# Two queues for the adjacency tiles of a graph network's first range, with the feature quarters behind them

## The chip, the cores and the metric

The kernel runs on one core of one Trainium2 chip. The metric is the time of one execution on the device in microseconds (us). It took 2988.14 us before the change (median of three runs, 2979.09 to 2988.84).

## The reference, cut to what matters

Four graph layers run over a dense 2708 x 2708 adjacency matrix (mostly zeros) and 2708 x 512 features, each with a residual and a layer norm. The change touches only how layer 0 starts:

```python
def _L0_gnn_ref(cur, incidence_m):
    mask = incidence_m > 0
    head = mask.astype(incidence_m.dtype)
    head = head / jnp.maximum(jnp.sqrt(jnp.sum(head * head, axis=-1, keepdims=True)), EPS)
    inc = incidence_m + head                      # needs the count of a whole row first
    edge_fea = inc @ cur
    edge_degree = jnp.sum(inc, axis=-1, keepdims=True)
    return edge_fea / edge_degree
...
x = _layernorm(x + _L0_gnn_ref(x, adj), axis=-1)  # layer 0; three more layers follow
```

What matters is the order of data. Before the first product of a row can be taken, the positive entries of that whole row have to be counted.

## The kernel before

The adjacency matrix is cut into four blocks "11", "12", "21", "22" of 1354 x 1354, and the features into four quarters B11, B12, B21, B22. Each block is worked on in ranges of up to 384 columns. The first range (256 columns) is `plain`, and for it a block has 11 tiles (ten of 128 rows and one of 74). Its loads, in the kernel before:

```python
def move(queue, dst, src):          # a tile's load; 74 rows go as 64 + 10, so 11 tiles are 12 issues
    ...
def load(ij, k, ...):
    ...
    move(nc.sync, t[:w, :n], adjT[j0 : j0 + w, hi * NH + R0 : hi * NH + R0 + n])
...
if plain:                           # (position in the list, length) of a block's 11 loads
    when = {"11": (-4.0, 0.2), "12": (-3.8, 0.2), "21": (-2.4, 0.4), "22": (-1.6, 0.4)}
    pw = {"11": (-0.9, 0.6), ...}   # the same for prep0 of each tile
```

The program is a list of events. `at(position, function)` enters one, the list is sorted by position, and each engine gets its instructions in the order that results. In the first part of the list this order is kept strictly; later events without the mark `True` may be taken earlier where nothing holds them.

The features of layer 0 and a bias vector of layer 1:

```python
def x0_load(k, s):
    if s == "B12":
        ...
        move(nc.sync, b12[k][: wt(k)], x_source(X0, k)[1])
    else:
        x_load(X0, k, s, nc.scalar if s == "B11" else nc.sync)
for k in range(KT):
    f = k / KT
    at(-5.0 + f, lambda k=k: x0_load(k, "B11"))
    at(-4.5 + 0.3 * f, lambda k=k: x0_load(k, "B21"))
    at(-4.0 + 0.3 * f, lambda k=k: x0_load(k, "B12"))
    ...
def start1():                       # layer 1; nothing holds it back, so the vector is loaded at the start
    W[1] = load_w(w_gcn)
    vec[1] = const.tile([P, D], F32, name="vec", tag="vec")
    nc.scalar.dma_start(out=vec[1], in_=bcast(b_gcn, D))
at(S[1] - 1.0, start1)
```

And the path from the tiles to the first product (h is the half of the rows, 0 first):

```python
for h, p, d in ((0, -3.7, 0.05), (1, 1.9, 0.055)):
    for i in range(NT):             # 22 tiles: 11 of block "h1", then 11 of "h2"
        at(..., lambda ...: count_mask(R0, n, h, i, a(), h == 0))   # h = 0 on VectorE, h = 1 on ScalarE
        at(..., lambda ...: count_tile(R0, n, h, i))                # TensorE: ones times mask
    at(..., lambda h=h: count_row(R0, n, h))                        # VectorE max, GpSimd power -1/2
    at(..., lambda h=h: spread_row(R0, n, h))

def spread_row(R0, n, h):
    ...                             # TensorE spreads 1/sqrt(count) over 128 partitions
    nc.scalar.copy(row[R0, h][:, :n], pr[:, :n])
def prep0(r, R0, n, h, hj, k, a):   # inc = adj + mask * row
    nc.vector.scalar_tensor_tensor(t[:w, :n], a[:w, :n], 0.0, row[R0, h][:w, :n], ALU.is_gt, ALU.mult)
    nc.vector.tensor_tensor(a[:w, :n], a[:w, :n], t[:w, :n], ALU.add)
```

GpSimd issues the count loads of the next range (`cl`, 192 KB each); it issues the first seven of them right after its part of `count_row`.

Of the kernel before, what the change touches and what calls it, by code (L numbers as in the profile page):

```python
# [27 lines left out]
NH = 1354  # L28
# [22 lines left out]
def wt(k):  # L51
    return min(P, NH - k * P) if k < KT else P
# [8 lines left out]
def gnn_kernel(ctx: ExitStack, tc: tile.TileContext, x, adjT, w_sa, a_sa, w_gcn, b_gcn, wab, bab, w_hop, w_out,  # L61
               b_out, out):
    nc = tc.nc
# [40 lines left out]
    X0 = [x[h * NH + k * P : h * NH + k * P + wt(k), :] for h in range(2) for k in range(KT)]  # L104
# [18 lines left out]
    def move(queue, dst, src):  # L123

        m = dst.shape[0]
        c = m - m % 16 if m > 16 else m
        queue.dma_start(out=dst[:c], in_=src[:c])  # L127
        if c < m:
            queue.dma_start(out=dst[c:m], in_=src[c:m])

    def ring_tile(nm):
        return pool.tile([P, 384], F32, name=nm, tag="ring", bufs=RING)
# [21 lines left out]
    def at(pos, fn, hold=False):  # L154

        def go():
            n = len(nc.cur_bb.bb.instructions)
            fn()
            held.update(range(n, len(nc.cur_bb.bb.instructions)))

        events.append((pos, len(events), go if hold else fn))
# [11 lines left out]
    def new_x(s, k):  # L173
        X[s, k] = place(s, *HOME[k])
        return X[s, k]
# [22 lines left out]
    def x_sums(k):  # L198
        w = wt(k)
        b = b12.pop(k)  # L200
        b11, b22 = X["B11", k], X["B22", k]
        nc.vector.tensor_tensor(new_x("T1", k)[:w], b[:w], b11[:w], ALU.subtract)
        nc.vector.tensor_tensor(new_x("T2", k)[:w], b22[:w], X["T1", k][:w], ALU.subtract)
        X["T3", k] = b
        nc.vector.tensor_tensor(b[:w], b22[:w], b[:w], ALU.subtract)
        X.pop(("B12", k), None)

    def x_last(k):
        w = wt(k)
        nc.vector.tensor_tensor(new_x("T4", k)[:w], X["B21", k][:w], X["T2", k][:w], ALU.subtract)  # L210

    def b12_tile(k):

        b12[k] = place("T3", *HOME[k])
        return b12[k]

    def x_source(src, k):

        lo, hi = src[k], src[KT + k]
        return lo[:, :HD], lo[:, HD:], hi[:, :HD], hi[:, HD:]  # L220

    def x_load(src, k, s, eng):
        w = wt(k)
        q = x_source(src, k)[("B11", "B12", "B21", "B22").index(s)]
        t = b12_tile(k) if s == "B12" else new_x(s, k)
        move(eng, t[:w], q)
# [74 lines left out]
    def sweep(base, nk, ranges, prep=None, extra=None, done=None, first=False, late=None, sums=False, save=False):  # L301
        A, spare = {}, {}
        for r, (R0, n) in enumerate(ranges):
            plain = first and r == 0
# [4 lines left out]
            def load(ij, k, R0=R0, n=n, r=r, plain=plain):  # L309
                hi, hj = int(ij[0]) - 1, int(ij[1]) - 1  # L310
                w = wt(k)
                if plain and ij == "22" and k >= KT - 8:

                    i = k - (KT - 8)
                    if i % 2 == 0:
                        spare[i // 2] = feat.tile([P, D], F32, name="aw", tag=f"w_{i // 2}")
                    t = spare[i // 2][:, i % 2 * HD : i % 2 * HD + n]
                else:
                    t = ring_tile("a" + ij)
                j0 = hj * NH + k * P  # L320
                move(nc.sync, t[:w, :n], adjT[j0 : j0 + w, hi * NH + R0 : hi * NH + R0 + n])
                A[r, ij, k] = t

            def prepare(ij, k, r=r, R0=R0, n=n):
# [13 lines left out]
            when = {"11": (-1.0, 1.0), "21": (-0.4, 1.0), "22": (0.75, 0.8), "12": (3.2, 1.0)}  # L338
            cw = {"s3": 0.3, "s1": 1.25, "s2": 2.1, "s4": 4.3}
            pw = {ij: (p + 0.3, f) for ij, (p, f) in when.items()}  # L340
            if plain:
                when = {"11": (-4.0, 0.2), "12": (-3.8, 0.2), "21": (-2.4, 0.4), "22": (-1.6, 0.4)}
                pw = {"11": (-0.9, 0.6), "12": (-0.3, 0.6), "21": (3.3, 0.9), "22": (4.1, 0.9)}
            for ij in ("11", "21", "22", "12"):
                for k in ks:
                    p, f = when[ij]
                    at(pb + p + f * k / nk, lambda ij=ij, k=k, load=load: load(ij, k))
                    if prep is not None:
                        p, f = pw[ij]
                        at(pb + p + f * k / nk, lambda ij=ij, k=k, prepare=prepare: prepare(ij, k))  # L350
            for k in ks if not plain else ():
                f = 0.75 * k / nk
# [305 lines left out]
    def x0_load(k, s):  # L658
        if s == "B12":
            X["B12", k] = b12_tile(k)  # L660
            move(nc.sync, b12[k][: wt(k)], x_source(X0, k)[1])
        else:
            x_load(X0, k, s, nc.scalar if s == "B11" else nc.sync)

    for k in range(KT):
        f = k / KT
        at(-5.0 + f, lambda k=k: x0_load(k, "B11"))
        at(-4.5 + 0.3 * f, lambda k=k: x0_load(k, "B21"))
        at(-4.0 + 0.3 * f, lambda k=k: x0_load(k, "B12"))
        at(-3.0 + 0.3 * f, lambda k=k: x0_load(k, "B22"))  # L670
        at(6.2 + 0.9 * f, lambda k=k: x_sums(k))
        at(7.5 + f, lambda k=k: x_last(k))
    at(9.3, start0)
    sweep(S[0], KT, RANGES0, prep=prep0, extra=extra0, done=done0, first=True, sums=True)


# [102 lines left out]
    def done1(p0, dp, last, R0, n, h, C, tiles):  # L779
        for i, (t, lo, w) in enumerate(tiles):  # L780
# [13 lines left out]
            at(p0 + 0.25 + dp * i, b)  # L794

    sweep(S[1], KT, RANGES, extra=extra1, done=done1, late=0.85, save=True)

    eps_col = const.tile([P, NT], F32, name="eps_col")
# [44 lines left out]
    def done2(p0, dp, last, R0, n, h, C, tiles):  # L843
        gots = []
        for i, (t, lo, w) in enumerate(tiles):
# [44 lines left out]
            at(q + 0.5 + 0.6 * dp * i, f)  # L890

    sweep(S[2], KT, RANGES, prep=prep2, extra=extra2, done=done2, sums=True)


# [332 lines left out]
```

## Time and profile before

| of the kernel before | value | where it is read |
|---|---|---|
| TensorE busy | 98% of 2983.9 us | busy times of the page |
| last mask of the first row ends | 19.50 us | timeline, the group at 18.94 |
| ScalarE's last load issue ends | 10.28 us | timeline |
| row copied on ScalarE | 21.61 us | timeline |
| first matmul of the layer | 22.95 us | timeline |
| second range starts | 120.50 us | timeline, the first matmul into `accu` |

TensorE is the bound for all but the start. The prediction below shows these lines; read them as one chain, in which each bracket names what the engine waited for. In them, `ACTq` is ScalarE's sequencer, which issues loads; `ACT` is its compute part. The two share one stream of instructions in order. `ACT_TABLE_LOAD`, called the table load here, stands once before ScalarE's first compute instruction and takes 1.28 us. PSUM is the memory in which TensorE's results lie.

### The profile page before, as it was taken

The page shows a single profiled execution, that of the slowest core. Times are in us where ns is not written, and L with a number is a line of the kernel's source. Part 1 is how long each engine was busy: PE and PEld are TensorE (multiplying, and loading weights), DVE is VectorE, ACT ScalarE, POOL GpSimd, SP SyncE. Part 2 cuts the span into 40 slices and gives each one's busy share as a digit, 9 for nine tenths or more (in the row PEclk, how much of TensorE's full clock was granted, in tenths as well). Part 3 has the DMA queues.
Part 4 walks back from the last instruction along what each step waited for, and adds up shares of the span by engine and source line. Part 5 has one row for each costly group of instructions (what it writes and reads, how often), then busy time and mean ns, then how long its engine had stood idle before and what let it go on. Part 6 is the DMA issues. An engine that isn't in the chain of part 4 may idle for free.

```text
span 2983.9 us, 37755 instructions
## 1 busy us (share of the span) xinstructions
PE 2930.5 (98%) x10982; PEld 1926.6 (65%) x10982; DVE 2191.4 (73%) x5376; ACT 596.3 (20%) x1145; POOL 692.6 (23%) x1240
## 2 busy tenths in 40 slices
PE   7999999999999999999999999999999999999998
PEld 6655666557665657766666666666666666665664
DVE  5889688556657675874686777867768877689786
ACT  4544200000144444551101000010000100100001
POOL 1423224233410101213112022020220322512112
PEclk9999999999999999999999999999999999999999
DMA  7665467586754333654676667565675666875562
GB/s 233 199 198 176 143 179 217 141 136 138 192 113 124 110 112 94 202 158 143 199 218 212 183 194 219 169 208 178 196 225 174 196 200 197 242 199 179 172 177 83
DMA packets 364119, 524.27 MB, mean 176 GB/s; under 512 B 57734, under 2 KB 312430, under 8 KB 363912
## 3 DMA queue, kind: packets, MB, share of 16 engines
q1 hardware_dynamic: 297556, 362.80, 43.4%
q0 software_dynamic: 57040, 148.22, 16.1%
q10 hardware_dynamic: 9316, 10.84, 1.2%
q8 instruction: 87, 1.43, 0.2%
q14 instruction: 120, 0.98, 0.1%
HBM read 431.26 MB, written 90.37 MB: 175 GB/s over the span
## 4 chain that ended last, share of the span: by engine, by line
PE 84%; issue 5%; DVE 4%; DMA 4%; ACT 1%; POOL 1%; SPq 1%; POOLq 0%; DVEq 0%; ACTq 0%
PE accc L1007 12%; PE accd L1007 12%; PE accu L1007 12%; PE ps_d L495 9%; PE accu L367 8%; PE accc L367 8%; PE accd L367 7%; PE acca L1007 6%; PE acca L367 4%; PE ps_n L1076 1%; PE accc L1012 1%; PE accu L1012 1%; PE accd L1012 1%; PE acca L1012 1%; SPq L127 1%
## 5 line engine op out<-in xcount | busy, mean ns | idle before, releaser
L967 DVE TENSOR_TENSOR z<-z 128x339 f32<-128x339 f32 (+1 forms) x966 | 468.8, 507 | 35.6 <-PE accu L1007 12.5
L1007 PE MATMUL accc<-z,t 128*128 128x338 f32 (+1 forms) x644 | 203.0, 447 | 0.0
L1007 PE MATMUL accc<-s,t 128*128 128x338 f32 (+1 forms) x644 | 197.9, 452 | 1.0 <-DVE s L967 1.0
L1007 PE MATMUL accd<-z,t 128*128 128x338 f32 (+1 forms) x644 | 195.2, 448 | 0.0
L1007 PE MATMUL accu<-z,t 128*128 128x338 f32 (+1 forms) x644 | 194.9, 448 | 0.0
L331 DVE TENSOR_TENSOR a<-a,a 128x384 f32<-128x384 f32 (+4 forms) x363 | 177.4, 511 | 13.9 <-PE accu L367 13.4
L1039 DVE TENSOR_TENSOR q<-q,accd 128x338 f32<-128x338 f32 (+1 forms) x112 | 56.4, 504 | 173.2 <-PE accd L1007 170.8
L1033 ACT COPY q<-accu 128x338 f32<-128x338 f32 (+1 forms) x84 | 34.3, 443 | 721.2 <-PE accu L1007 721.2
L449 POOL TENSOR_TENSOR rstd<-rstd,neg_half 128x1 f32<-128x1 f32 (+3 forms) x92 | 61.5, 668 | 495.1 <-DVE rstd L448 494.2
L967 DVE TENSOR_TENSOR s<-z 128x338 f32<-128x338 f32 (+1 forms) x322 | 154.2, 505 | 23.4 <-PE accc L1007 20.6
L1007 PEld LDWEIGHTS accc<-z,t 128*128 128x128 f32 x644 | 121.4, 189 | 61.3 <-issue 2.2
L1007 PEld LDWEIGHTS accc<-s,t 128*128 128x128 f32 x644 | 121.6, 192 | 59.8 <-issue 2.5
L1007 PEld LDWEIGHTS accu<-z,t 128*128 128x128 f32 x644 | 121.0, 190 | 59.0 <-issue 1.5
L1007 PEld LDWEIGHTS accd<-z,t 128*128 128x128 f32 x644 | 120.8, 190 | 58.3 <-issue 1.9
L757 DVE SCALAR_TENSOR_TENSOR deg<-a,deg 128x384 f32<-128x384 f32 (+5 forms) x168 | 81.5, 504 | 68.1 <-DMA a<-in_adjT 67.8
L127 POOL DMA_DIRECT2D Y<-y x102 | 55.3, 543 | 280.3 <-ACT y L1089 192.8
L822 ACT ACTIVATE e<-row,neg_s 128x384 f32<-128x384 f32 (+5 forms) x176 | 100.5, 571 | 86.5 <-DVE e L824 23.9
L824 DVE TENSOR_TENSOR e<-e,f 128x384 f32<-128x384 f32 (+5 forms) x176 | 87.3, 504 | 25.3 <-ACT f L823 24.2
L823 ACT ACTIVATE f<-row,neg_s 128x384 f32<-128x384 f32 (+5 forms) x176 | 99.9, 567 | 12.6 <-PE accc L367 6.4
L127 POOL DMA_DIRECT2D As<-a x132 | 71.2, 543 | 107.1 <-DVE a L331 48.8
L1089 ACT COPY y<-ps_n 128x512 f32<-128x512 f32 (+2 forms) x48 | 28.0, 584 | 322.3 <-issue 175.6
L495 PE MATMUL ps_d<-w,q 128*128 128x512 f32 (+2 forms) x192 | 88.1, 604 | 3.5 <-DVE q L1145 3.4
(655 smaller groups left out, 6173.5 us busy)
## 6 DMA issues: line engine op xcount, KB each, us to landing
z<-As SPq DMA_DIRECT2D x320, 169.5 KB
z<-As SPq DMA_DIRECT2D x320, 169.0 KB
a<-in_adjT SPq DMA_DIRECT2D x240, 192.0 KB
z<-in_adjT SPq DMA_DIRECT2D x240, 169.5 KB
z<-in_adjT SPq DMA_DIRECT2D x240, 169.0 KB
a<-in_adjT SPq DMA_DIRECT2D x120, 165.0 KB
cl<-in_adjT POOLq DMA_DIRECT2D x80, 192.0 KB, 4.5
a<-in_adjT SPq DMA_DIRECT2D x113, 128.0 KB
```

The source lines that it names most:

```text
L127: queue.dma_start(out=dst[:c], in_=src[:c])
L331: nc.vector.tensor_tensor(A[r, dst, k][:w, :n], A[r, a, k][:w, :n], A[r, b, k][:w, :n], op)
L367: nc.tensor.matmul(B[home, c][:, :n], X[STAT[p], k][:w, c * P : (c + 1) * P], A[r, MOV[p], k][:w, :n], start=bool(start and k == k0), stop ...
L449: nc.gpsimd.tensor_tensor(rstd[:w, 1:2], rstd[:w, 0:1], neg_half[:w], ALU.pow)
L495: nc.tensor.matmul(o, lhs(c), r, start=c == 0 and n == 0, stop=c == DC - 1, skip_group_check=True)
L757: nc.vector.scalar_tensor_tensor(d[:w, :n], a[:w, :n], 0.0, d[:w, :n], ALU.not_equal, ALU.add)
L822: nc.scalar.activation(e[:w, :n], row[R0, h][0][:w, :n], AF.Exp, bias=neg_s[:w, t : t + 1])
L823: nc.scalar.activation(f[:w, :n], row[R0, h][1][:w, :n], AF.Exp, bias=neg_s01[:w, t : t + 1])
L824: nc.vector.tensor_tensor(e[:w, :n], e[:w, :n], f[:w, :n], ALU.min)
L967: nc.vector.tensor_tensor(d[:, :n], Z[x + (k,)][:, :n], Z[y + (k,)][:, :n], op)
L1007: nc.tensor.matmul(B[home][:, :n], stat(v, k), a[:, :n], start=bool(start and k == 0), stop=k == nk - 1, skip_group_check=True)
L1012: nc.tensor.matmul(B[home][:, :n], groups[st, "R"][0][:w, c * P : (c + 1) * P], Z[p, 2, 0][:w, :n], start=False, stop=True, skip_group_che ...
```

## The change

The intent: block "12", the second half of what the first row needs, no longer queues behind block "11" on SyncE. ScalarE issues it at the same time. The quarters come behind: B11 behind block "11" on SyncE, and B21 behind block "12" on ScalarE.

```diff
-                move(nc.sync, t[:w, :n], adjT[j0 : j0 + w, hi * NH + R0 : hi * NH + R0 + n])
+                q = nc.scalar if plain and ij == "12" else nc.sync
+                move(q, t[:w, :n], adjT[j0 : j0 + w, hi * NH + R0 : hi * NH + R0 + n])
...
-                when = {"11": (-4.0, 0.2), "12": (-3.8, 0.2), "21": (-2.4, 0.4), "22": (-1.6, 0.4)}
+                when = {"11": (-4.0, 0.2), "12": (-4.0, 0.2), "21": (-2.4, 0.4), "22": (-1.6, 0.4)}
...
-            x_load(X0, k, s, nc.scalar if s == "B11" else nc.sync)
+            x_load(X0, k, s, nc.scalar if s == "B21" else nc.sync)
...
-        at(-5.0 + f, lambda k=k: x0_load(k, "B11"))
+        at(-4.6 + 0.3 * f, lambda k=k: x0_load(k, "B11"))
```

## The prediction

> **What bounds the kernel now.** I read the page's busy shares and 40 slices first, to see whether anything but TensorE can matter:
>
> ```profile
> PE 2930.5 (98%) x10982; PEld 1926.6 (65%) x10982; DVE 2191.4 (73%) x5376; ACT 596.3 (20%) x1145; POOL 692.6 (23%) x1240
> ...
> PE   7999999999999999999999999999999999999998
> ...
> DMA  7665467586754333654676667565675666875562
> ```
>
> TensorE is busy for 2930.5 of 2983.9 us. Its only slice below 9 tenths, before the last, is the first one, 75 us long. So a change to the first loads is worth what it moves TensorE's first real matmuls, provided nothing later takes it back. The sums of waits from 100 us to the end show only about 22 us of TensorE idle, the longest single wait 3.8 us; 3.5 us of them are for transfers, the rest for results that follow TensorE's own work. A shift of TensorE's work before 100 us therefore reaches the end one for one.
>
> Next the timeline of the first 23 us, which is the path to the first real matmul. Columns: start, duration, engine, line, operation, tiles, and in brackets the idle time before it with its releaser.
>
> ```profile
> 0.74 1.36 ACTq L127 DMA_DIRECT2D B11A<-in_x  x3
> ...
> 9.92 0.36 ACTq L686 DMA_DIRECT2D vec<-in_b_gcn  x1
> ...
> 10.31 1.28 ACT L566 ACT_TABLE_LOAD   x1 [10.31 <-DMA B11D<-in_x]
> ...
> 13.26 0.29 DVE L528 TENSOR_SCALAR mask<-a 74x256 bf16<-74x256 f32 x1 [0.55 <-DMA a<-in_adjT]
> ...
> 14.73 1.25 DVE L528 TENSOR_SCALAR mask<-a 128x256 bf16<-128x256 f32 x4 [1.18 <-DMA a<-in_adjT]
> ...
> 18.94 0.56 DVE L528 TENSOR_SCALAR mask<-a 128x256 bf16<-128x256 f32 x2 [0.21 <-DMA a<-in_adjT]
> ...
> 19.80 0.22 DVE L553 TENSOR_SCALAR r<-cnt 128x1 f32<-128x1 f32 x2 [0.31 <-PE cnt L541]
> ...
> 20.11 0.72 POOL L555 TENSOR_TENSOR r<-r,neg_half 128x2 f32<-128x2 f32 x1 [18.80 <-DVE r L553]
> ...
> 20.88 0.69 PE L563 MATMUL pr<-ident,r 128*128 128x128 f32 x2 [1.12 <-DMA B21B<-in_x]
> ...
> 21.61 0.37 ACT L566 COPY row<-pr 128x256 f32<-128x256 f32 x1 [10.02 <-PE pr L563]
> ...
> 22.01 0.42 DVE L578 SCALAR_TENSOR_TENSOR s<-a,row 128x256 f32<-128x256 f32 x1 [1.99 <-ACT row L566]
> ...
> 22.95 0.80 PE L377 MATMUL acca<-a,B11A 128*128 128x256 f32 x1 [1.38 <-DVE a L579]
> ```
>
> The reader should see one chain. 22 adjacency tiles (11 of block "11", then 11 of block "12") land; VectorE makes a mask of each; TensorE counts; VectorE, GpSimd and TensorE turn the count into a row; ScalarE copies that row out of PSUM (21.61); VectorE prepares the first tile (22.01); TensorE starts the layer at 22.95. From the end of the last mask (18.94 + 0.56 = 19.50) to the copy it takes 2.11 us. ScalarE also issued twelve loads, from 0.74 to 10.28, and did its table load at 10.31: long over when the row came at 21.6.
>
> Then stretches, to see what the loads were limited by (columns: stretch, length, busy us of TensorE, its weight load, VectorE, ScalarE, GpSimd, granted clock, DMA share, GB/s):
>
> ```profile
> 2.00:10.00 8.00, 1.49 (x14) 0.92 (x14) 2.35 (x8) 0.00 (x0) 0.00 (x0) 1.00 0.98 311
> ...
> 14.00:22.00 8.00, 3.04 (x24) 1.75 (x24) 3.42 (x13) 0.37 (x1) 1.89 (x3) 1.00 0.84 251
> ```
>
> With two queues issuing, the DMA engines are 98% busy and move 311 GB/s. With SyncE alone they move 251 GB/s at 84%: SyncE's issues come one per 0.47 us, and 131 KB / 0.47 us is 279 GB/s at the very most.
>
> Last, TensorE's idle time after its start, up to 100 us. These two lines are the larger ones:
>
> ```profile
> 59.59 0.20 PE L541 MATMUL cnt<-ones_bf,mask 74*128 74x1 bf16 x2 [0.55 <-ACT mask L531]
> ...
> 90.07 0.23 PE L541 MATMUL cnt<-ones_bf,mask 128*128 128x1 bf16 x3 [2.28 <-ACT mask L531]
> ```
>
> There are also 0.31, 0.27 and 0.35 us at 54.11, 58.84 and 84.55. All come from ScalarE's masks.
>
> **What the Trainium skill says.** "DMA: Bandwidth & Descriptors", section "Issuing engines are not separate DMA queues", says that DMAs from the scalar, sync and gpsimd engines run on the same 16 DMA engines and interleave, and that issuing from several saves only the sequencer's issue time. The trace agrees: 251 against 311 GB/s is the whole difference, and at 98% busy there is no third step. "Perfetto Trace Analysis", section "DMA Instruction — HWDGE (DVE, Sync)", puts the start that the profiler reports after all semaphores are satisfied and has the sequencer free for the next instruction only at the reported end. So an issue that waits blocks its engine without a busy record. The trace agrees: ScalarE's twelve issues cost 0.33 to 0.54 us each, about 5 us, but are spread over 9.54 us. "ScalarE: Activation LUTs", section "What ACT_TABLE_LOAD costs", gives about 1283 ns; the trace has 1.28 us.
>
> **The change, part by part.** The instructions of VectorE, TensorE and GpSimd keep their order; only queues and tile names differ.
>
> (1) Loads of block "12" move from SyncE to ScalarE; the first feature quarter (B11) goes from ScalarE to SyncE and the second (B21) from SyncE to ScalarE. Each quarter or block is 12 issues. SyncE loses 12 net, ScalarE gains 12: it now has the bias vector, 12 of "12" and 12 of B21, 25 in all. The bytes are the same.
>
> (2) Block "11" stays first on SyncE, and ScalarE's traffic competes as before, so I leave its last mask at 13.26 us. Block "12" no longer stands behind it. ScalarE's queue carried 1.65 MB (B11 and the vector) until about 13 us before; now its first 1.65 MB are the vector and "12", so "12" is there at about 13 us too. VectorE then goes through the 11 masks at the rate of the burst in the timeline, four in 1.25 us: 11 x 0.31 = 3.4 us, ending at 13.55 + 3.4 = 17.0 instead of 19.50. Gain on this branch 2.5 us; the row would be ready for ScalarE at 17.0 + 2.1 = 19.1.
>
> (3) But the copy of that row is on ScalarE, behind all 25 issues and the table load. In the built program each of ScalarE's loads waits for the one four places before it on the same queue. The last issue can start only when load 21 (third tile of B21's third group) has landed. In bytes: vector 0.262 + "12" 1.386 + eight tiles of B21 1.049 = 2.70 MB on this queue. I summed the trace's packets per queue: 1.27 MB by 10 us, and half of 311 GB/s, some 158 KB per us, since 2 us. So 2.70 MB at 10 + 1.43 / 0.158 = 19.0 us, and with 0.7 us from last byte to the next issue (seen at B11's end) 19.7. The last issue takes 0.54, the table load 1.28: 21.5. From the issue rhythm instead (0.83 us per load in the trace before, from the fifth to the twelfth, less two small loads) I get 20.8; from 3.6 us per four loads, 22.3. I take 21.5 for the start of the copy, range 20.8 to 22.3, against 21.61.
>
> (4) So the branch that was on the path gets 2.5 us shorter and ScalarE's issue queue takes its place: the first matmul moves by 0.1 us (0.8 earlier to 0.7 later).
>
> (5) Loads after that are ahead: by 20 us the two queues together have moved about 0.6 MB more than before (10 us at 60 GB/s), so later quarters and blocks land some 2.5 us sooner. None is waited for by TensorE before 100 us. ScalarE's masks of the second half start after the copy of the first accumulators at 44.95, which waits for TensorE, and then run every 0.755 us without a break to 56.97: limited by ScalarE, not by loads. So the 1.13 us of gaps between 54 and 60 us stay. The 2.28 us at 90.07 wait for a count tile whose load GpSimd issues behind a store of normalized rows (83.81), and that follows transposes on TensorE (78.64): it moves along with TensorE.
>
> Sum: 0.1 us of 2988, within 1 us either way.
>
> **Rivals.** (a) ScalarE is not in the way: its loads land faster than half of the rate, or the copy's wait is shorter. Then 2.5 us come through, 2985.6. For it: DMA in that stretch could give ScalarE more than half while SyncE waits on shared semaphores. Against: 98% busy engines have little to give. (b) The chain of waits runs back from 51.70 us through SyncE's issues at one per 0.47 us. If this is real, 12 fewer issues give 12 x 0.47 = 5.6 us, 2982.5. Against it: ScalarE's masks around 51.70 keep their 0.755 us rhythm, so that landing only coincides. (c) The row being ready earlier, GpSimd starts its seven count loads (1.38 MB, issued right after its part of the row) near 18.3 instead of 20.77, in the middle of ScalarE's last loads. Before, at 23 to 29 us, these took some 220 of 330 KB per us. If they hit ScalarE's last megabyte, the copy comes 1 to 3 us later: 2990. They start landing about 2.2 us after the issue, at 20.5, so mostly too late for that. (d) A cold or warm TensorE: 12 first matmuls took 5.3 us, 0.44 each, twice their later spacing; the idle time before them is as long after the change, so no difference.
>
> **Time, range and chances.** Mechanism: 2988.14 - 0.1 = 2988.0. The three runs of before reach from 2979.09 to 2988.84, a spread of 9.8 us, far above the effect, and the low one lies on the side where also (a) and (b) lie; I put the median at 2987.5. For 8 in 10 I take 2978.5 (the low run) to 2993 (the high run plus (c)). Two per cent is 60 us, over half of the whole stretch before 100 us, so faster and slower get 0.01 each.
>
> **What would show it.** Right: last mask at about 17.0; a table load near 20.2 instead of 10.31, with the copy directly behind it, released by ScalarE's own queue and not by TensorE; the first matmul of the layer between 22.1 and 23.7; DMA share above 0.9 from 10 to 20 us. Wrong if the table load comes before 18.5 (then (a)), if masks end later than 18.5, if the gap near 59 or that near 90 is gone (then my view that they move along with TensorE fails, and 1 to 3 us more are gained), or if waits after 100 us grow by more than 2 us in sum.

## The result, and the profile after

The kernel after took 2989.61 us (median of six runs, 2985.16 to 2995.02), the kernel before 2986.40 in its six runs (2979.09 to 2991.34). The ratio is 1.0014, with an interval of 0.9995 to 1.0034. Ratios here are the mean time of one kernel's runs over that of the other's of the same rounds, so they are not quite the ratio of the medians quoted. Five more runs gave 1.0016 (1.0003 to 1.0028): the change costs some 0.15%, about 4.5 us. The time is inside the predicted range; the way there isn't what was predicted.

The page after, busy times and slices:

```profile
PE 2926.8 (98%) x10982; PEld 1926.1 (65%) x10982; DVE 2191.0 (73%) x5376; ACT 596.1 (20%) x1145; POOL 692.7 (23%) x1240
...
PE   6999999999999999999999999999999999999998
```

Still 98%. Only the first slice differs, 6 tenths where it was 7: less TensorE work in the first 75 us.

The timeline after answers to the chain shown of before (start, duration, engine, line, operation, tiles, count, idle time and releaser):

```profile
0.74 0.41 ACTq L687 DMA_DIRECT2D vec<-in_b_gcn  x1
1.18 10.35 ACTq L127 DMA_DIRECT2D a<-in_adjT  x11
...
13.99 2.51 DVE L529 TENSOR_SCALAR mask<-a 74x256 bf16<-74x256 f32 x12 [1.11 <-DMA a<-in_adjT]
...
17.12 0.72 POOL L556 TENSOR_TENSOR r<-r,neg_half 128x2 f32<-128x2 f32 x1 [15.82 <-DVE r L554]
17.79 3.91 POOL L127 DMA_DIRECT2D cl<-in_adjT  x7
...
17.90 0.69 PE L564 MATMUL pr<-ident,r 128*128 128x128 f32 x2 [1.12 <-DMA B11B<-in_x]
19.31 1.20 ACTq L127 DMA_DIRECT2D B21D<-in_x  x2
...
23.05 0.47 ACTq L127 DMA_DIRECT2D B21R<-in_x  x1
24.39 0.32 ACTq L129 DMA_DIRECT2D B21R<-in_x  x1
24.74 1.28 ACT L567 ACT_TABLE_LOAD   x1 [24.74 <-DMA B21C<-in_x]
26.03 0.37 ACT L567 COPY row<-pr 128x256 f32<-128x256 f32 x1
...
27.38 5.49 PE L378 MATMUL acca<-a,B11A 128*128 128x256 f32 x12 [8.79 <-DVE a L580]
```

The masks end at 13.99 + 2.51 = 16.50 us instead of 19.50, and the row lies in PSUM at 17.90 + 0.69 = 18.59. Nothing takes it from there for 7.4 us. ScalarE is to copy it, but its stream still holds loads of B21, and each waits for an earlier one to land. Between 20.51 and 23.05 the timeline shows nothing on ScalarE at all: a waiting issue leaves no busy record. Only after the last issue (24.71) come the table load and the copy. TensorE starts at 27.38 us, 4.4 us later than before. In the second trace of the same kernel it was 26.29.

The loads' first 30 us in 40 slices of 0.75 us, before and then after: busy share of the DMA engines, and GB/s.

```profile
DMA  0038999999999856768999976868969999799999
GB/s 0 0 59 292 363 358 366 279 258 337 305 332 317 260 175 212 194 171 227 291 246 243 294 210 215 276 210 253 298 182 309 344 270 253 264 331 381 374 342 352
```

```profile
DMA  0027699999999999788969999998898999996692
GB/s 0 0 83 138 141 232 378 378 291 309 255 275 301 337 341 298 195 220 238 325 143 219 301 313 348 236 325 270 229 260 295 363 391 393 367 261 155 160 291 74
```

See the fourth to sixth slices (2.25 to 4.5 us). Before, they moved 292, 363 and 358 GB/s; after, 138, 141 and 232, although the engines were 7, 6 and 9 tenths busy. This is the bias vector, now in front of all of ScalarE's loads. It is one row of 2 KB read 128 times, and its packets took 157 ns each on average (168 to 190 in the other traces with it in front), against a median of 46 ns for the 1 KB packets of the adjacency tiles and the quarters. Before, it came behind B11, around 11 to 14 us, at 101 ns a packet.

The windows after that answer to the two shown of before (columns as there):

```profile
2.00:10.00 8.00, 1.28 (x12) 0.79 (x12) 1.76 (x6) 0.00 (x0) 0.00 (x0) 1.00 0.91 268
...
14.00:22.00 8.00, 3.12 (x26) 1.85 (x26) 2.73 (x14) 0.00 (x0) 4.58 (x8) 1.00 0.96 270
```

And TensorE's two gaps that the prediction said would move along:

```profile
63.81 0.20 PE L542 MATMUL cnt<-ones_bf,mask 74*128 74x1 bf16 x2 [0.55 <-ACT mask L532]
...
94.21 0.23 PE L542 MATMUL cnt<-ones_bf,mask 128*128 128x1 bf16 x3 [2.01 <-ACT mask L532]
```

They are there, 4.1 to 4.2 us later, and about the same length.

One thing has to be explained before experiments are compared: the two profiled runs have equal spans, 2983.9 us before and 2983.8 after. I matched TensorE's matmuls by their number. At the 1200th, 2000th, 3000th, 4000th, 4800th and 6000th the kernel after lags by 4.1, 3.3, 1.6, 0.9, 3.6 and 1.2 us, at the last by nothing. The trace's clock records say why it varies. Up to the last matmul the clock was halved for 27.31 us in before and for 20.48 in after, in stretches of 3.41 or 6.83 us whose number differs from run to run. Half of the difference, 3.4 us, is what before lost more. (The records also hold a last stretch, behind the last matmul, that runs past the end of the span; with it they sum to 35.97 and 27.66 us, which is where the 36.0 and 27.7 of the next expectation come from.) With what each had lost up to the place taken off, the lag is 2.6 to 4.1 us at all these matmuls, the last included.

"TensorE: Matmul & The Clock Gate" in the Trainium skill, section "What's actually happening", tells of a free-running window of 3413 ns after which the clock changes between half and full, and the lengths agree. The thirteen traces other than a_table's hold 73 stretches before the last matmul. Each begins behind 3.41 us in which TensorE had idled for 1.75 us or more, but not each such wait has one behind it: in before the wait of 2.28 us at 90.07 has, that of 2.09 at 787.22 has not. The two traces of the changed kernel lost 10.2 and 13.7 us up to the last matmul. So two profiles of one kernel can differ by 3.4 us in this alone, and for effects of this size only the early landmarks and repeated timings count.

### The profile page after: what moved, and what is told of

It is laid out like the page before. It is cut to its first block, busy times and chain, and to the rows that moved or that the text cites. A ratio compares the mean times of both kernels' runs of the same rounds, so it can differ in the third digit from the quotient of the medians.

```text
span 2983.8 us, 37754 instructions
## 1 busy us (share of the span) xinstructions
PE 2926.8 (98%) x10982; PEld 1926.1 (65%) x10982; DVE 2191.0 (73%) x5376; ACT 596.1 (20%) x1145; POOL 692.7 (23%) x1240
## 4 chain that ended last, share of the span: by engine, by line
PE 85%; DMA 5%; DVE 4%; issue 3%; POOL 1%; SPq 1%; ACT 1%; POOLq 0%; ACTq 0%; DVEq 0%
PE accd L1008 11%; PE accc L1008 11%; PE accu L1008 11%; PE ps_d L496 10%; PE accu L368 8%; PE accc L368 8%; PE accd L368 8%; PE acca L1008 6%; PE acca L368 4%; DMA a<-in_adjT 1%; PE accd L1013 1%; PE accu L1013 1%; PE accc L1013 1%; PE ps_n L1077 1%; PE acca L1013 1%
## 5 line engine op out<-in xcount | busy, mean ns | idle before, releaser
L825 DVE TENSOR_TENSOR e<-e,f 128x384 f32<-128x384 f32 (+5 forms) x176 | 87.4, 504 | 25.8 <-ACT f L824 24.7
L579 DVE SCALAR_TENSOR_TENSOR s<-a,row 128x384 f32<-128x384 f32 (+5 forms) x168 | 82.9, 506 | 17.2 <-ACT row L567 15.6
```

Source lines behind the costliest of these rows:

```text
L825: nc.vector.tensor_tensor(e[:w, :n], e[:w, :n], f[:w, :n], ALU.min)
```

## The experiments

My theory after the result: the row copy stands in ScalarE's stream behind B21's loads (step 3 of the prediction), and the loads land later than I reckoned for two reasons, the vector in front of them and GpSimd's count loads, which now start at 17.79 and meet ScalarE's last ones. The rivals: TensorE waits for something else, such as B11, which is now on SyncE behind block "11"; or only one of the two reasons is real; or the lower rate has a third cause. Each kernel was timed in the same rounds and on the same chip as before (five rounds; the last has a single run). They gave correct results.

The landmarks of all the traces, in us. "Row copied" is the start of the copy. The start of the second range holds what the half clock had cost by then: nothing in after_again, a_cl_behind, a_vec_late and b_vec_late, 3.4 us in a_b21_sync, 5.1 in best_again, 1.7 in all others, before and after too.

| kernel | last mask ends | last ScalarE issue ends | row copied | first matmul of the layer | second range starts | ratio to before (95%) |
|---|---|---|---|---|---|---|
| before | 19.50 | 10.28 | 21.61 | 22.95 | 120.50 | 1 |
| after | 16.50 | 24.71 | 26.03 | 27.38 | 124.64 | 1.0014 (0.9995 to 1.0034) |
| after_again | 16.59 | 23.62 | 24.95 | 26.29 | 121.77 | 1.0016 (1.0003 to 1.0028) |
| a_copy_dve | 17.36 | 25.66 | 19.47 | 20.86 | 118.68 | 0.9990 (0.9977 to 1.0004) |
| a_cl_behind | 16.75 | 23.26 | 24.58 | 25.93 | 120.58 | 1.0006 (0.9994 to 1.0019) |
| a_vec_late | 15.52 | 21.68 | 23.01 | 24.36 | 118.75 | 1.0016 (1.0003 to 1.0030) |
| a_cl_vec | 15.71 | 20.89 | 22.22 | 23.56 | 120.74 | 0.9989 (0.9962 to 1.0015) |
| a_b21_sync | 17.21 | 12.71 | 19.33 | 20.67 | 118.96 | 1.0001 (0.9976 to 1.0026) |
| a_b21_vec | 15.99 | 11.08 | 18.11 | 19.46 | 116.69 | 0.9992 (0.9965 to 1.0019) |
| best_inter | 13.24 | 11.36 | 15.36 | 16.71 | 115.98 | 0.9984 (0.9960 to 1.0007) |
| best_again | 12.76 | 10.76 | 14.87 | 16.21 | 118.93 | 0.9999 (0.9982 to 1.0015) |
| best_pool | 13.24 | 10.95 | 15.36 | 16.70 | 115.10 | 1.0007 (0.9991 to 1.0023) |
| b_vec_late | 18.99 | 10.46 | 21.11 | 22.45 | 117.50 | 0.9998 (0.9982 to 1.0013) |
| a_table | 16.76 | 27.77 | 27.80 | 29.15 | 125.86 | one run, not used |

### after_again: the same kernel once more

No edit; it shares its rounds with the next three.

> The changed kernel once more, for five rounds on the chip that the next three share. Theory: the copy of the count row waits behind ScalarE's own 25 load issues and its table load, so the layer's first matmul comes near 27.4 us instead of 22.95, TensorE keeps that loss (124.6 against 120.5 us at the start of the second range), and the time is about 4 us (0.14%) longer than before. Rival: the two profiled spans are equal (2983.8 and 2983.9 us), so nothing is lost in the end and the ratio is 1.000. The theory says that the span was equal only because the run of before had 36.0 us at half clock and the run of after 27.7.

The median was 2988.73 us, against 2983.19 for before (nine runs). The first matmul came at 26.29 us, so the late start repeats, and it varies by a microsecond between executions.

### a_copy_dve: the first row copied by VectorE

```diff
-        nc.scalar.copy(row[R0, h][:, :n], pr[:, :n])
+        if (R0, h) == (RANGES0[0][0], 0):
+            nc.vector.tensor_copy(row[R0, h][:, :n], pr[:, :n])
+        else:
+            nc.scalar.copy(row[R0, h][:, :n], pr[:, :n])
```

> The changed kernel with the copy of the first count row on VectorE, nothing else. Theory (ScalarE's queue is the wait): the row is in PSUM at 18.6 us as before this edit, the copy follows at once, first matmul of the layer near 19.9 us, 7.5 us sooner than in the changed kernel and 3 us sooner than before; time about 3 us below before, 7 below the changed kernel. Rival (the loads of the first feature quarter, not the copy, are late): the first matmul stays past 24 us and waits for a load of B11.

From the timeline of this kernel:

```profile
19.47 0.42 DVE L568 COPY row<-pr 128x256 f32<-128x256 f32 x1 [1.58 <-PE pr L564]
...
20.86 4.49 PE L378 MATMUL acca<-a,B11A 128*128 128x256 f32 x12 [1.44 <-DVE a L583]
...
25.35 0.31 ACTq L129 DMA_DIRECT2D B21R<-in_x  x1
```

The copy is now released by TensorE's `pr`, and TensorE starts at 20.86 us, 5.4 to 6.5 earlier than in after, although ScalarE's last issue ends no sooner (25.66). This shows that ScalarE's stream was the wait, and that B11 on SyncE was not. The whole time was 2980.66 us against 2983.19, a ratio of 0.999 that can't be told from 1. Against the changed kernel it can: in the same rounds the mean was 2981.2 us, that of after_again 2988.8, and the 7.6 us between them (7 were expected; a 95% interval from the five times of each is some 3 to 12) show that what the row's wait cost was in the whole time too.

### a_cl_behind: GpSimd's count loads held until the copy is done

```diff
         nc.scalar.copy(row[R0, h][:, :n], pr[:, :n])
+        if (R0, h) == (RANGES0[0][0], 0):
+            nc.gpsimd.tensor_tensor(gate_x[:, 0, 0:1], row[R0, h][:, 0:1], neg_half, ALU.pow)
```

The added instruction on GpSimd reads the copied row, and so makes what GpSimd issues after it wait. What it writes is written anew before layer 1 reads it.

> The changed kernel with GpSimd's first seven count loads held back until the row copy is done (a one-column operation on GpSimd reads the row first). Theory (these loads take the DMA engines from ScalarE's last loads): B21's last tiles land without them, table load at about 22.2 instead of 24.7 us, first matmul near 24.8 instead of 27.4, still later than before. Rival (the two queues alone are too slow, or the vector in front is the whole cause): first matmul stays within 0.5 us of 27.4.

From the timeline:

```profile
23.29 1.28 ACT L567 ACT_TABLE_LOAD   x1 [23.29 <-DMA B21D<-in_x]
...
25.77 3.98 POOL L127 DMA_DIRECT2D cl<-in_adjT  x7
```

The count loads are issued at 25.77 instead of 17.79, and the table load comes at 23.29 instead of 24.74 and 23.65 in the two traces of after: 0.4 to 1.5 us earlier. Less than expected (22.2); GpSimd's loads are a part of the delay and the smaller one.

### a_vec_late: the bias vector not loaded at the start

```diff
         W[1] = load_w(w_gcn)
+
+    def start1v():
         vec[1] = const.tile([P, D], F32, name="vec", tag="vec")
...
     at(S[1] - 1.0, start1)
+    at(S[1] - 1.0, start1v, True)
```

> The changed kernel with the bias vector's broadcast load at its place in the program (about 750 us later) instead of at the head of ScalarE's queue. Theory (the vector delays the first tiles): the first mask starts near 3.7 instead of 5.48 us, everything in the first stretch about 1.5 us sooner, first matmul near 25.8. Rival (the vector only takes its 0.26 MB, 0.8 us at 311 GB/s): first mask later than 4.6 us and the first matmul at 26.6 or later.

The table load, from its timeline:

```profile
21.72 1.28 ACT L567 ACT_TABLE_LOAD   x1 [21.72 <-DMA B21D<-in_x]
```

It is 1.9 to 3.0 us earlier, and the first matmul is at 24.36 where 25.8 was expected. The fourth to sixth slices of the loads are back at 306, 346 and 232 GB/s. So the vector costs more than its bytes: 0.26 MB are 0.8 us at the 311 GB/s of all queues, and 1.7 us at the 158 KB per us that the prediction gave ScalarE's queue. That loads which are earlier meet fewer of GpSimd's isn't the whole reason: with GpSimd held back in both, the table load comes at 23.29 with the vector (a_cl_behind) and at 20.92 without (a_cl_vec, below), 2.4 us apart. The time is no better than that of after (1.0016; the means of the two in the same rounds are 0.1 us apart), which the start doesn't explain.

### a_cl_vec: both of these

The edit is that of a_cl_behind and that of a_vec_late.

> Both edits at once on the changed kernel: bias vector late, and GpSimd's first count loads behind the row copy. This is the traffic that the prediction had in mind for its estimate, less the vector. If the two effects are separate they add (about 2.6 + 1.6 us): table load near 20.5, copy near 21.8, first matmul near 23.2 us, level with the 22.95 of before, time within 1.5 us of before. If they overlap, or if a third cause is left, the first matmul stays at 24.5 or later.

```profile
20.92 1.28 ACT L567 ACT_TABLE_LOAD   x1 [20.92 <-DMA B21D<-in_x]
22.22 0.37 ACT L567 COPY row<-pr 128x256 f32<-128x256 f32 x1
```

The two causes together move the table load by 2.7 to 3.8 us, to 20.92, near the 20.2 that the prediction had. But they don't account for its error, because the 20.2 had the vector's 0.26 MB in it. Without them its sum reads 10 + (2.44 - 1.27) / 0.158 = 17.4 us, and with 0.7 and 0.54 a table load at 18.6. Measured against this, 2.3 us remain for a third cause: ScalarE's queue moved 1.29 MB from 10 to 20 us in this trace, 129 KB per us and not 158. Why it did is not shown. On this chip before took 2993.17 us (11 runs, 2984 to 3008), so the ratio of 0.9989 says little.

### a_b21_sync: B21 on SyncE, so ScalarE has only block "12" and the vector

```diff
-            x_load(X0, k, s, nc.scalar if s == "B21" else nc.sync)
+            x_load(X0, k, s, nc.sync)
```

> The changed kernel with the second feature quarter (B21) issued by SyncE after the first, so that ScalarE issues only the vector and block 12. Theory: ScalarE is done at about 12.5 us, its table load is over before 14, the copy starts when the row is ready (18.6), first matmul near 19.9, about 3 us sooner than before; time 3 us below before. Rival (SyncE, with 12 more issues in front, now makes the later blocks late): TensorE gets new waits for loads between 20 and 100 us and the gain at 125 us is below 1 us.

```profile
12.75 1.28 ACT L567 ACT_TABLE_LOAD   x1 [12.75 <-DMA a<-in_adjT]
...
19.33 0.37 ACT L567 COPY row<-pr 128x256 f32<-128x256 f32 x1 [5.30 <-PE pr L564]
...
20.67 4.55 PE L378 MATMUL acca<-a,B11A 128*128 128x256 f32 x12 [1.38 <-DVE a L580]
```

With twelve issues fewer, the table load happens at 12.75 in idle time, the copy waits for TensorE as before the change, and the first matmul is at 20.67. This is a second, independent test that shows ScalarE's stream as the wait. But the time is the same (1.0001), and a new wait of 1.96 us appears on TensorE at 49.92, for a mask of ScalarE.

### a_b21_vec: B21 on SyncE and the vector late

The edit is that of a_b21_sync and that of a_vec_late.

> As the run before, with the bias vector late as well. Theory: both gains; block 11 lands about 1.5 us sooner, the masks end near 15.0, the row copy near 17.1, first matmul near 18.4, 4.5 us sooner than before; time 4.5 us below before. If the first matmul is not at least 1 us sooner than with the vector in front, the vector does not matter on this path.

The first matmul is at 19.46 us, 3.5 us ahead of before, and the second range starts at 116.69, 3.8 ahead. The ratio is 0.9992. In its trace TensorE waits 2.16 us at 49.05 for a mask, and 10.18 us in one go before 785.56, where before waited 2.09 us before 787.22. So in this execution a later wait took most of the lead.

### best_inter and best_again: the masks in the order in which the tiles land

With two queues, tiles of "11" and "12" land in turn, but the masks go through "11" first. This version is a_b21_vec with this edit:

```diff
-                for i in range(NT):
+                for m in range(NT):
+                    i = m if h else m // 2 + KT * (m % 2)
...
-                    at(pb + p + d * (i - 2 * h), ...count_mask...)
-                    at(pb + p + d * i, ...count_tile...)
+                    at(pb + p + d * (m - 2 * h), ...count_mask...)
+                    at(pb + p + d * m, ...count_tile...)
```

> As the run before, and the masks and counts of the first half taken in the order in which the tiles now arrive (one of block 11, one of block 12, in turn) instead of all of 11 and then all of 12. Theory: the burst of 11 masks at the end (2.5 us in the changed kernel) shrinks to one or two masks, the row comes about 2 us sooner, first matmul near 16.5, 6.5 us sooner than before; time 6 us (0.2%) below before. Rival: the first matmul then waits for B11's first tile, or TensorE is held up later by SyncE's loads, and less than half of the further 2 us is left at 125 us.

> The last kernel of the call before (block 12 alone on ScalarE, vector late, masks in the order of arrival) once more, because its call showed times of before from 2984 to 3008 us and its interval included 1. First matmul near 16.7 us again, TensorE waits some 2.8 us for ScalarE's mask near 48 us, second range near 116 us. Theory: 3 to 6 us below before (ratio 0.998 to 0.999). If the ratio is 1.000 or above over both calls, an early start in this stretch is worth nothing.

From the timeline of best_inter:

```profile
15.36 0.37 ACT L567 COPY row<-pr 128x256 f32<-128x256 f32 x1 [2.69 <-PE pr L564]
...
16.71 4.94 PE L378 MATMUL acca<-a,B11A 128*128 128x256 f32 x12 [1.38 <-DVE a L580]
...
48.47 0.21 PE L542 MATMUL cnt<-ones_bf,mask 128*128 128x1 bf16 x2 [2.80 <-ACT mask L532]
```

This is the start that the change was after: 16.71 us, 6.2 us ahead of before. At 48.47 TensorE waits 2.80 us for a mask of the second half. ScalarE, which makes it, has idled 3.11 us before 47.55 for the tile, which doesn't come that early; of the lead, 4.5 us are left at the second range (115.98). The two timings were 0.9984 (0.9960 to 1.0007) and 0.9999 (0.9982 to 1.0015). Both intervals hold 1. So no gain is shown for the best start that I could build, and a small one isn't excluded. In best_again the first matmul was 6.7 us ahead, the second range only 1.6: its waits for masks before it sum to 6.5 us against 3.8 in before, and two stretches of half clock, from 48.8 and 89.7 us, cost 5.1 us against 1.7.

### best_pool: quarter B12 issued by GpSimd, so that later tiles come sooner

```diff
-            move(nc.sync, b12[k][: wt(k)], x_source(X0, k)[1])
+            move(nc.gpsimd, b12[k][: wt(k)], x_source(X0, k)[1])
...
-        at(-4.0 + 0.3 * f, lambda k=k: x0_load(k, "B12"))
+        at(-3.45 + 0.3 * f, lambda k=k: x0_load(k, "B12"))
```

These two edits are on top of best_inter.

> The same, with the third feature quarter (B12) issued by GpSimd after its part of the row instead of by SyncE: SyncE's later blocks come 12 issues (5.6 us) sooner. Theory (the 2.8 us wait near 48 us is for block 22, late in SyncE's order): that wait and the smaller ones at 40 and 44 us go, the second range starts near 112 to 113 us, time 7 to 8 us below before. Rival: TensorE waits for B12 instead (needed from about 37 us), or GpSimd's later count loads come too late, and the second range starts no earlier than 115 us.

The wait near 48 us is gone (0.39 us at 48.05), but 2.95 us appear at 84.67, and the second range starts at 115.10, not at the 112 to 113 expected. Later the lead goes. TensorE's wait lines:

```profile
688.31 0.59 PE L789 MATMUL pz<-wab_sb,P1c 128*128 128x2 f32 x2 [5.10 <-DVE P1c L409]
...
786.36 1.01 PE L789 MATMUL pz<-wab_sb,P1c 128*128 128x2 f32 x4 [5.67 <-DVE P1c L409]
```

The same line of before, near the second of these, in its own trace:

```profile
787.22 0.72 PE L784 MATMUL pz<-wab_sb,P1c 128*128 128x2 f32 x4 [2.09 <-DVE P1c L408]
```

TensorE leaves this wait at 786.36 in best_pool and at 787.22 in before: of 5.4 us of lead at the second range, 0.9 are left, and up to there before had lost 1.1 us more to the half clock. All waits of TensorE after 100 us sum to 32.2 us in best_pool and 22.2 in before. The ratio was 1.0007.

### b_vec_late: the vector late in the kernel before

The edit is that of a_vec_late, in the kernel before.

> The kernel before with only the bias vector's load moved to its place in the program. There the vector was the last of ScalarE's loads, not the first. Theory (the broadcast slows whatever is in flight with it): the dip between 10 and 14 us (201 GB/s against 311) goes and the first matmul comes 0.5 to 1.5 us sooner, 21.5 to 22.5. Rival (only its place at the head of the queue hurt): first matmul at 22.95 within 0.3 us.

The first matmul came at 22.45 instead of 22.95, and the ratio is 0.9998. Between 10 and 14 us, where the vector had landed in before, the engines moved 216 GB/s at a share of 0.75 (201 at 0.70 before), so the dip there isn't the vector's. In the order of before the vector costs next to nothing; it is costly only in front of the loads that the first row needs.

### a_table: the table loaded early

```diff
+    at(-4.55, lambda: nc.scalar.copy(gate_x[:, 1, 0:1], ones_f))
```

A small copy between ScalarE's two groups of loads draws the table load forward, off the end of the chain.

> The changed kernel with a one-column copy on ScalarE between its two groups of loads, so that the table load is done there. Theory: the row copy follows ScalarE's last load issue directly instead of 1.3 us later; the first matmul comes 1.3 us sooner for the same end of the issues (about 1.7 us instead of 3.0 after the end of the last issue). The issues of B21 themselves start about 1.3 us later, so their end may move by up to as much.

```profile
27.45 0.32 ACTq L129 DMA_DIRECT2D B21R<-in_x  x1
27.80 0.37 ACT L567 COPY row<-pr 128x256 f32<-128x256 f32 x1 [13.60 <-DMA B21D<-in_x]
```

The row copy does follow the last issue after 0.03 us, without the 1.28 us table load between. But the issues end at 27.77, 3 to 4 us later than in after, so the copy came later, not earlier. Why putting one instruction among the issues delays them by more than its own time isn't settled; this was one look.

## Why the prediction was right or wrong

The time lay in the range, but more by its width than by insight: 14.5 us, set by the spread of before and by rival (c). The middle, a change of 0.1 us, was not what happened. Of the four signs that the prediction named for being right, two came true, masks near 17.0 (16.50) and a DMA share above 0.9 from 10 to 20 us (0.95). The table load (24.74 for 20.2) and the first matmul (27.38 for 22.1 to 23.7) didn't. Of the steps:

**Step 1, the count of issues: right.** The timeline after shows the vector, twelve of block "12" and twelve of B21 on ScalarE. (Before, they were thirteen with the vector, not the twelve that the prediction counts on its timeline.)

**Step 2, masks end at 17.0: nearly right.** They ended at 16.50. The last mask of block "11" came later than the 13.26 assumed, at 13.99, and the burst behind it was quicker: twelve in 2.51 us, 0.21 each, not 0.31. Four masks in 1.25 us had still included waits for tiles.

**Step 3, ScalarE's queue takes the place: the mechanism right, the size wrong. This is the step that failed.** It put the copy at 21.5 us, range 20.8 to 22.3; it started at 26.03 (24.95 in the second trace). That the copy waits for ScalarE's own issues is shown twice: moving the copy (20.86) or the issues (20.67) brings the first matmul forward by five to seven microseconds. Summing each queue's packets in the trace of after shows which terms were too small:

| term of step 3 | predicted | in the trace | difference, us |
|---|---|---|---|
| bytes landed at 10 us | 1.27 MB, as before | 1.16 MB, the vector being in front | 0.11 / 0.158 = 0.7 |
| rate of ScalarE's queue to 20 us | 158 KB/us | 1.37 MB in 10 us, 137 KB/us | 1.54 / 0.137 - 1.54 / 0.158 = 1.5 |
| 2.70 MB landed, from 20 us on | not needed | the last 0.165 MB take until 23.3 at 35 to 70 KB/us, beside GpSimd's loads | 3.3 - 0.165 / 0.137 = 2.1 |
| from landing to the last issue | 0.7 us | 24.39 - 23.29 = 1.1 | 0.4 |
| last issue | 0.54 us | 0.32 | -0.2 |
| sum | | | 4.5 = 26.03 - 21.5 |

The first and third terms have experiments behind them: without the vector in front the table load comes 1.9 to 3.0 us earlier, with GpSimd held back 0.4 to 1.5, with both 2.7 to 3.8. The second term is only partly explained. The rate of all queues from 10 to 20 us was 272 GB/s in after, at a DMA share of 0.95, and in a_cl_vec, with both causes gone, it was still 257. Half of the 311 that I carried over from another stretch, where the share was 0.98, was too much for this one, so a high busy share was no sign of a high rate; why stays open. "DMA: Bandwidth & Descriptors" in the Trainium skill, section "Queues, rings and completion order", says that each DMA engine takes turns between the queues that have work, packet by packet. I had taken two turns in a circle of two; with GpSimd there are three, and its queue got more than half: 266 of 396 KB in the microsecond from 24 us. In the trace GpSimd's packets are of 3072 and 4608 bytes, those of the other two queues of 1024, so even turns by packet would give it, as an estimate from the mean of 4.1 KB, 4.1 of 6.1 KB or two thirds, which is that share.

**Step 4, the first matmul moves by 0.1 us: wrong with step 3**, by the same amount: +4.4 and +3.3 us in the two traces.

**Step 5, the later gaps: right, the reason given for the loads wrong.** By 20 us the queues should have moved 0.6 MB more than before. From the rates of the two stretches of 10 us it was 0.07 MB: 251 and 231 GB/s before, 217 and 272 after. So nothing was ahead. The three gaps near 60 us were 0.31, 0.27 and 0.55 us, 1.13 in sum as before, and the one at 90.07 came at 94.21. In the kernels with B21 on SyncE a gap of 2.0 to 2.8 us appeared near 48 us, but for best_pool. So the gaps move with TensorE when it is late, but when it is early there is a limit: the tiles of the second half.

**The premise, one for one to the end: held for the loss, not shown for gains.** The timings of after (+0.14% and +0.16%, about 4.5 us) fit a start 3.3 to 4.4 us later, and waits after 100 us didn't grow (21.4 us against 22.2). But starts 3.5 to 6.7 us earlier gave ratios of 0.9984 to 1.0007. In single traces I can show where such a lead went: 10.18 us of wait near 785 us in a_b21_vec, and 10.8 us in the two waits near 688 and 786 us in best_pool, where before waits 4.8 us for the same result. In the chain of waits of before, transfers end one after another between 682 and 775 us, which suggests that a stretch limited by transfers there doesn't begin earlier when TensorE does. That is argued, not tested; best_inter and best_again lost no more there than before did (4.3 and 3.6 us), so it doesn't explain why they gained so little. Nor does the start explain a_vec_late, which timed like after. Between a_copy_dve and after_again the premise held: 7.6 us of time for 5.4 to 6.5 us at the first matmul.

**The rivals.** (a), ScalarE not in the way, is rejected: the copy waited for it. (b), a gain of 5.6 us through SyncE's shorter chain of issues, didn't come; waits after the start stayed the same, so nothing hung on it while TensorE was late. With an early start it did count: best_pool, with twelve issues less on SyncE, lost the wait near 48 us (2.80 to 0.39). (c), GpSimd's count loads on ScalarE's last megabyte, was given as "mostly too late for that". It was real, with a share of 0.4 to 1.5 us. (d), the clock of TensorE at its start: the first twelve matmuls took 5.49 us in both first traces, so no difference between them.

## What to carry to other kernels

A load issued by an engine that also computes puts everything behind it in that engine's stream behind the landing of earlier loads where these loads wait for one another, as here, so count the loads between an engine and its next piece of critical work, and reckon with the slowest thing in front of them. When such a queue becomes the limit, its rate has to be taken from its own stretch, with every other queue that will be active then, and not as half of the best rate seen elsewhere. And a shorter start isn't a shorter run until the later waits have been looked at in the trace: here leads of 3.5 to 6.7 us at the first matmul left no gain that the timings, uncertain by 5 to 8 us, could show.

## What the Trainium skill lacked or had wrong

- "DMA: Bandwidth & Descriptors", section "Issuing engines are not separate DMA queues", says that issuing from several engines saves only issue time. It doesn't warn of the cost: with 25 issues on ScalarE, its copy of a row that was ready at 18.59 us started at 26.03.
- The section "Queues, rings and completion order" of the same page has the DMA engines take turns by packet. How bytes divide when queues carry different shapes isn't told; here GpSimd's queue, with packets of 3072 and 4608 bytes, moved 266 of 396 KB in one microsecond, beside two other queues with packets of 1024.
- No page that I found gives the cost of a load that reads one 2 KB row for all 128 partitions: its packets took 157 ns on average (101 ns in another place in the kernel before), against a median of 46 ns for 1 KB packets.
- "TensorE: Matmul & The Clock Gate" gives the window of 3413 ns, which agrees with the half-clock stretches of 3.41 and 6.83 us. What it lacks is how much they come to, and differ, in a run at 98% busy: 20.5 to 27.3 us of half clock up to the last matmul in the traces of before and after, 3.4 us of time between two executions of one kernel. It also lacks that a stretch can begin behind a window that is only partly idle: here 1.75 us of idle time in the 3.41 us before were the least.
